# Layer 3 by row chunks, loads in pieces, value sums on VectorE and weight sums through DRAM in a four-layer graph network

## The chip, the cores and the metric

The kernel runs on one core of a Trainium2 chip. The metric is the device time of the run in microseconds; the median of several runs counts. A profiled execution gives the times of the single instructions.

## The reference

32 graphs of 512 nodes with 256 features each go through four layers. After every layer comes a residual and a layer norm over the features. The adjacency `adj` (512x512 for each graph) is the same in all layers, everything is in float32.

```python
# layer 0: x + MLP of the aggregated features
h = (1.0 + eps) * x + einsum('bnm,bmd->bnd', adj, x)
y = relu(h @ W1 + b1) @ W2 + b2
# layer 1: graph attention, 4 heads, only where adj > 0.5
h = einsum('bnd,dhf->bnhf', x, W)
e = leaky_relu(e_dst[:, :, :, None] + e_src[:, :, None, :], 0.2)
attn = softmax(where(adj > 0.5, e, -1e9)); y = einsum('bhij,bjhf->bihf', attn, h) + bias
# layer 2: 8 heads, log(adj + 1e-6) added to the scores
attn = softmax(q @ k.T / sqrt(32) + log(adj + 1e-6)); y = (attn @ v) @ Wo.T + bo
# layer 3: one head
s = (x @ W) @ x.T * adj; s = where(nodemask, s, -1e30); y = softmax(s) @ x
# after each of them
x = layernorm(x + y)
```

## The kernel before

The work is cut by graph. `prepare()` loads and turns the weights once and works out a bound that decides between `fast_path` and a general path (the general path isn't taken with these inputs). `graph(g)` then describes the four layers of one graph as small steps. 512 nodes are four chunks of 128 rows (`NC = 4`), 256 features are two chunks (`DC = 2`).

Nothing in `graph` is issued when it is described. A step has a name, an engine, an assumed duration, the steps it comes after, and the buffers it takes and frees. The class `Plan` orders them all: it keeps a simulated clock for each engine and picks among the ready steps, within a small look-ahead (`ahead`), the one whose due time is first. The due time is `max(g - 1, 0) * period` less the longest remaining chain of the step. `run` tries a few settings, takes the one that ends first by the plan's own clock, and emits the instructions of all engines in that order. Each engine then executes its own list strictly in that order, and waits where a semaphore isn't there yet. So the order of TensorE, VectorE, ScalarE, GpSimd and of SyncE's transfers is fixed when the kernel is built. Up to six graphs are under way at the same time (`"live": 6`), and steps of different layers of different graphs lie beside each other.

The buffers are a stock in SBUF by size: `B` (a 128x4x512 tile), `C` (128x4x256), single ones such as `ATd`, `dT`, `rdT`, `node`, and the eight banks of PSUM (`p`). SyncE's transfers are steps of an engine "sp" of 0.1 us, and the transfers themselves are steps of fixed length on an assumed queue.

The places that matter here, by their step names:

- Layer 0: `ldx` and `ldA` load x and the adjacency of a graph in one transfer each (L614, L619). `at` turns the adjacency on TensorE (L639), `atd` and `ate` copy it to SBUF (VectorE L643, ScalarE L647). `h` aggregates (L671), `f` and `y` are the MLP (L694, L713).
- The weights are loaded by ScalarE's queue (L320), 15 transfers at the start.
- Layer 1: `xt1` turns x (L739), and ScalarE's copy of it also sums each feature over the nodes (`xs`). `v1` makes the values (L760). `R`, `Rt`, `Re`, `Rd` make a row of exponentials, turn it, write it to DRAM (`R_dram`, L809) and read it back to all partitions (`R_bc`, L811). `z` and `zm` make the unnormalised attention (L850, L861), `o1` multiplies it with the values (L884). `hs` multiplies the feature sums with the weights (L822: four matmuls of one column, in float32 two instructions each), `hse` scales it, and `oe` adds it to the output. The sums of the weights, `d1`, come from an accumulating DMA over the chunks and one group of matmuls with ones (L930); `de` copies them to `dT` (L941), and `yt` turns, chunk by chunk, two blocks of the output and a block of `dT` (L949 to L951), so that `yn` can take the reciprocal of 4 columns (L957) and scale (L959).
- Layer 2: `s` are scores with four heads in the four row tiles of the array (L1046), `e` and `m` the exps and the products with the adjacency (L1059, L1068), `n` the outputs (L1104, column tiles). The weights of a group of four heads are summed over the chunks with two rounds of accumulating DMAs (`collect`, L1079) and then one group of matmuls with ones, `d2` (L1128). `rc` takes reciprocals (L1143), `yd` scales (L1147), `p` is the output projection (L1176).
- Layer 3: `ldA3` loads adjacency and node mask again (L1190, L1192). `i` and `t` are the similarities (L1215, L1229), `ta`, `tb`, `te` the mask, maximum and exp of one row chunk (L1243, L1249, L1257). The transposes `u` (L1274) take column block m of all four row chunks, so they come after all four exps; `w` multiplies (L1301), `wx` adds to x (L1315), then follow the norm and `out` (L1330).

Of the kernel before, what the change touches and what calls it, by code (L numbers as in the profile page):

```python
# [11 lines left out]
I32 = mybir.dt.int32  # L12
# [34 lines left out]
class Plan:  # L47
# [7 lines left out]

    HOP = {"pe": 0.2, "act": 0.15, "dve": 0.13, "pool": 0.05, "sp": 0.05}
# [3 lines left out]
        "": {"": 0.0, "row": 0.1, "c32": 0.1, "c64": 0.1},  # L60
        "row": {"": 0.13, "row": 0.1, "c32": 0.2, "c64": 0.2},
# [72 lines left out]
    def order(self, period, ahead, window, stay, shift=0.0, seed=0):  # L134
# [10 lines left out]
        rng = random.Random(seed)  # L145
        moved = {n: rng.uniform(-shift, shift) for n in [*self.steps[0], *self.steps[-1]]}
# [10 lines left out]
        while low < len(self.steps):  # L157
            found = []
            for (g, name), t in ready.items():
# [8 lines left out]
                else:  # L168
                    due = max(g - 1, 0) * period - self.left[g][name] + moved[name] + stay * change
# [47 lines left out]
def fast_path(  # L217
# [57 lines left out]
    wg_sb = const.tile([P, DC, VW], F32, name="wg_sb")  # L275
    ab_off = const.tile([P, 2, H1], F32, name="ab_off")
# [6 lines left out]
    def blk(i):  # L283
# [4 lines left out]
        "B": 14, "C": 13, "p": 8,  # L288

        "live": 6, "L0": 1, "L1": 2, "L2": 2, "L3": 1, "AT": 4, "zs": 7,  # L290
        "ATd": 1, "edge": 1, "dT": 1, "tmp": 2, "rdT": 2, "node": 1,
# [7 lines left out]
    def row(name, n):  # L299
        return tuple(f"{name}{i}" for i in range(n))  # L300


    def prepare():
# [10 lines left out]
        def load(name, us, *transfers, take=()):  # L314


            @step(f"ld_{name}", "act", 0.5 * len(transfers), take=take)
            def _():
                for transfer in transfers:
                    nc.scalar.dma_start(*transfer())  # L320

            @step(name, "q3", us, (f"ld_{name}",))
            def _():
                pass
# [4 lines left out]
        def transposed(name, w):  # L329
# [4 lines left out]
            load(f"raw{name}", 1.2, raw, take=(f"C=raw{name}",))  # L334
# [18 lines left out]
        load("eps", 2.0, lambda: (eps_bc, row_bcast(eps0, 1)))  # L353
# [3 lines left out]
        def _():  # L357
# [3 lines left out]
        load(  # L361
            "w1", 3.0, lambda: (w1_sb, rows(w1)), lambda: (b1_sb, b1.rearrange("(c p) -> p c", p=P))
        )
# [8 lines left out]
        load("bias", 3.0, *(bias_rows(k, b) for k, b in enumerate((b2, gbias, bo))))  # L372

        def vector(name, a):
# [6 lines left out]
        load(  # L381
            "wg", 3.0,
            lambda: (wg_sb[:, :, :D], wg.rearrange("(c p) h f -> p c (h f)", p=P)),
            vector("a0", a_src), vector("a1", a_dst), take=("C=a0", "C=a1"),
        )

        @step("wa", "dve", 3.2, ("wg",), take=("C=prod",), free=("prod", "a0", "a1"))
        def _():
            for k in range(2):
# [6 lines left out]
                )  # L396

# [125 lines left out]
    def graph(g):  # L523
        plan.graph()
        slot = plan.slot[-1]
        t = {"g": g}
# [4 lines left out]
        def mid(key, shape, name):  # L531
            return sb.tile(shape, F32, tag=f"C{slot[key]}", name=f"{name}_{g}")

# [24 lines left out]
        def norm_stats(n, c):  # L558
            nc.vector.bn_stats(t[f"st{n}"][:, c, :], t["x"][:, c, :])  # L559
            nc.vector.bn_aggr(t[f"mv{n}"][:, c, :], t[f"st{n}"][:, c, :])  # L560
# [5 lines left out]
        def norm_steps(n, after):  # L566


            @step(f"ve{n}", "dve", 0.09, after)
            def _():  # L570
                t["ve"] = little([P, NC], f"ve{n}")
                nc.vector.tensor_scalar_add(t["ve"], t[f"mv{n}"][:, :, 1], LN_EPS)  # L572

            @step(f"dev{n}", "pool", 1.1, (f"ve{n}",))
            def _():
                t["rstd"] = little([P, NC], f"rstd{n}")
                nc.gpsimd.tensor_tensor(t["rstd"], t["ve"], nhalf, ALU.pow)  # L577

            @step(f"sh{n}", "dve", 0.09, (f"dev{n}",))
            def _():  # L580
# [40 lines left out]
        @step("ld", "q0", 8.0, ("ldA",))  # L621
        def _():
            pass
# [1190 lines left out]
```

## Time and profile before

| | us |
|---|---|
| median of 3 runs | 3010.78 |
| lowest, highest | 3010.47, 3017.16 |
| profiled execution | 3013.04 |
| its span in the trace | 3011.3 |
| TensorE busy in it | 2944.1 |
| VectorE, ScalarE, GpSimd busy | 2009.7, 1946.5, 619.8 |
| mean granted TensorE clock | 0.991 |

The span is from the first to the last instruction of the trace; 1.7 us of the profiled execution lie around it. The profile gives for a group of instructions its line in the kernel, engine, operation, output and input names, shapes and count, then the busy time, the mean duration of one, and the idle time of that engine just ahead of it with what ended it. Durations of matmuls overlap, so the distance from the start of one group to the start of the next says what a group costs TensorE.

### The profile page before, as it was taken

To read this page: it belongs to the slowest core of one execution; us is meant where nothing else is said; L and a number is where in the kernel's file an instruction comes from. 1 tells how busy PE (TensorE), PEld (TensorE's weight loads), DVE (VectorE), ACT (ScalarE), POOL (GpSimd) and SP (SyncE) were. 2 spreads that over 40 slices of the span, in tenths; PEclk is the share of its full clock that TensorE was granted. 3 is DMA by queue.
4 is the path that set the end of the run, shared out by engine and by line. 5 is a ranking of instruction groups with operands and counts; after the bars stand their busy time and mean duration, and the time that the engine had idled before them with its cause. 6 is when DMAs were issued, how large, how long until landed. Compare 5 with 4: busy or idle time off the path is not lost. (4 is left out here: it accounts for less than half of the span.)

```text
span 3011.3 us, 40812 instructions
## 1 busy us (share of the span) xinstructions
PE 2944.1 (98%) x15053; PEld 1703.7 (57%) x15053; DVE 2009.7 (67%) x3935; ACT 1946.5 (65%) x3849; POOL 619.8 (21%) x686
## 2 busy tenths in 40 slices
PE   7899999999999999999999999999999999999996
PEld 5544655555565555565555565555565555565544
DVE  1467576676676676676676676676676676676874
ACT  2667566767666767666767666767666767666762
POOL 0222122112222112222112222112222112222210
PEclk9999999999999999999999999999999999999998
DMA  4579767788887788887787887787877787887963
GB/s 152 125 173 194 154 137 172 160 180 177 180 168 165 161 182 174 180 166 170 160 184 171 181 166 168 160 187 168 180 163 173 160 189 168 177 168 150 199 133 79
DMA packets 159782, 500.82 MB, mean 166 GB/s; under 512 B 13132, under 2 KB 48728, under 8 KB 130904
## 3 DMA queue, kind: packets, MB, share of 16 engines
q0 software_dynamic: 78336, 352.36, 62.0%
q1 hardware_dynamic: 77824, 142.88, 13.8%
q10 hardware_dynamic: 3416, 2.90, 0.3%
q8 instruction: 121, 1.98, 0.3%
q14 instruction: 85, 0.70, 0.1%
HBM read 179.06 MB, written 17.05 MB: 65 GB/s over the span
## 5 line engine op out<-in xcount | busy, mean ns | idle before, releaser
L1068 DVE SCALAR_TENSOR_TENSOR z<-AT,z 128x1024 f32<-128x1024 f32 x512 | 610.9, 1217 | 273.2 <-ACT z L1059 272.7
L1059 ACT ACTIVATE z<-s 128x512 f32<-128x512 f32 x1024 | 551.3, 611 | 268.3 <-PE s L1046 268.1
L1143 DVE RECIPROCAL rdT<-rdT 128x256 f32<-128x256 f32 x128 | 218.3, 1728 | 316.2 <-ACT rdT L1136 316.2
L861 DVE SCALAR_TENSOR_TENSOR z<-z,T,edge 128x512 f32<-128x512 f32 x512 | 357.8, 747 | 62.2 <-ACT z L850 62.0
L850 ACT ACTIVATE z<-R_bc,nT,S 128x512 f32<-128x512 f32 x512 | 382.1, 819 | 17.8 <-DMA R_bc<-R_dram 17.8
L1079 POOL DMA_DIRECT2D z<-z x192 | 169.5, 883 | 992.2 <-PE o_ps L1104 268.7
L590 ACT ACTIVATE x<-x,shift,rstd 128x256 f32<-128x256 f32 x512 | 295.4, 602 | 108.0 <-DVE shift L582 108.0
L912 POOL DMA_DIRECT2D z<-z x256 | 228.8, 1033 | 467.5 <-DMA z<-z 265.2
L1046 PE MATMUL s<-qT,kT 32*128 32x512 f32 x2048 | 291.8, 634 | 0.1
L577 POOL TENSOR_TENSOR rstd<-ve,nhalf 128x4 f32<-128x4 f32 x128 | 134.7, 1052 | 696.9 <-DVE ve L572 671.6
L1104 PE MATMUL o_ps<-z,v 128*32 128x512 f32 x2048 | 260.5, 601 | 0.3 <-ACT z L1059 0.3
L694 PE MATMUL h1T_ps<-hT,w_sb 128*128 128x512 f32 x512 | 240.0, 604 | 0.0
L1229 PE MATMUL s<-xT,iT 128*128 128x512 f32 x512 | 237.4, 598 | 0.0
L1301 PE MATMUL o_ps<-x,eT 128*128 128x256 f32 x1024 | 237.4, 385 | 0.0
L713 PE MATMUL y_ps<-w_sb,h1T 128*128 128x256 f32 x1024 | 232.4, 381 | 2.2 <-ACT h1T L700 2.2
L884 PE MATMUL o_ps<-z,v 128*64 128x512 f32 x1024 | 230.8, 602 | 1.5 <-DVE z L861 1.5
L1301 PEld LDWEIGHTS o_ps<-x,eT 128*128 128x128 f32 x1024 | 189.5, 190 | 68.1 <-issue 22.8
L713 PEld LDWEIGHTS y_ps<-w_sb,h1T 128*128 128x128 f32 x1024 | 194.6, 191 | 52.8 <-issue 20.7
L671 PE MATMUL hT_ps<-AT,x 128*128 128x384 f32 (+2 forms) x768 | 210.1, 383 | 8.8 <-ACT AT L647 8.8
L559 DVE BATCH_NORM_STATS2 st<-x 128x6 f32<-128x256 f32 x512 | 211.9, 414 | 5.6
L1046 PEld LDWEIGHTS s<-qT,kT 32*128 32x128 f32 x2048 | 93.5, 183 | 158.7 <-issue 66.8
L694 PEld LDWEIGHTS h1T_ps<-hT,w_sb 128*128 128x128 f32 x512 | 90.5, 190 | 122.0 <-issue 112.8
(145 smaller groups left out, 4261.5 us busy)
## 6 DMA issues: line engine op xcount, KB each, us to landing
z<-z POOLq DMA_DIRECT2D x192, 1024.0 KB, 8.2
A<-in_adj_dram SPq DMA_DIRECT2D x64, 1024.0 KB, 11.0
z<-z POOLq DMA_DIRECT2D x128, 512.0 KB, 8.0
x<-biases POOLq DMA_DIRECT2D x96, 512.0 KB, 9.6
R_bc<-R_dram SPq DMA_DIRECT2D x32, 1024.0 KB, 4.5
z<-z POOLq DMA_DIRECT2D x128, 256.0 KB, 7.7
x<-in_x_dram SPq DMA_DIRECT2D x32, 512.0 KB, 6.0
out_dram<-x SPq DMA_DIRECT2D x32, 512.0 KB, 3.8
```

The source lines that it names most:

```text
L590: nc.scalar.activation(t["x"][:, c, :], t["x"][:, c, :], AF.Identity, bias=t["shift"][:, c : c + 1], scale=t["rstd"][:, c : c + 1],)
L694: nc.tensor.matmul(ph, w1_sb[:, d, blk(f)], t["hT"][:, d, :], start=(d == 0), stop=(d == DC - 1))
L713: nc.tensor.matmul(py[:, j, :], t["h1T"][:, f, blk(2 * c2 + j)], w2_sb[:, f, :], start=(f == 0), stop=(f == HC - 1),)
L850: nc.scalar.activation(t[f"e{h}"][:, c, :], t["Rbc"][:, h, :], AF.Relu, bias=t["nT"][:, h, c : c + 1], scale=t["S"][:, h, c : c + 1],)
L861: nc.vector.scalar_tensor_tensor(z, z, t["T"][:, h, c : c + 1], t["edge"][:, c, :], op0=ALU.add, op1=ALU.mult)
L884: nc.tensor.matmul(po[j * F1 : (j + 1) * F1, :], t["v"][:, c, h * F1 : (h + 1) * F1], t[f"e{h}"][:, c, :], start=(c == 0), stop=(c == NC - 1),
L1046: nc.tensor.matmul(pk, t["k"][hs, o, blk(c)], t["q"][hs, o, :], start=True, stop=True)
L1059: nc.scalar.activation(t[f"E{k}"][:, j, :], t[f"ps{k}{j}"], AF.Exp, scale=QSCALE)
L1068: nc.vector.scalar_tensor_tensor(z, t["AT"][:, c, None, :].to_broadcast([P, 2, N]), ADJ_EPS, z, op0=ALU.add, op1=ALU.mult,)
L1104: nc.tensor.matmul(t[f"n{o}"][32 * j : 32 * j + 32, :], t["v2"][:, c, o * P + F2 * j : o * P + F2 * (j + 1)], t[f"E{k}"][:, j, :], start=( ...
L1229: nc.tensor.matmul(pt, t["iT"][:, d, blk(c)], t["xT3"][:, d, :], start=(d == 0), stop=(d == DC - 1),)
L1301: nc.tensor.matmul(py[:, j, :], t["eT"][:, m, blk(2 * c2 + j)], t["x"][:, m, :], start=(m == 0), stop=(m == NC - 1),)
```

## The change

1. The plan gets a stock `D` of 19 strips of 128x512; `B` falls from 14 to 11 buffers and `C` from 13 to 12. Both loads of the adjacency, the broadcast row R, layer 3's z and its transposes, `rdT`, `dT`, `ATd` and the mask live in strips.
2. The adjacency is loaded in four pieces in layer 0 and in layer 3, R in four pieces by head. `at` works on a row chunk (all column blocks of one chunk) rather than on a column block. SyncE's issues are steps of 0.4 us, and their transfers share one assumed queue `q1`.
3. The large weights are loaded by SyncE after the first graph's adjacency and x; ScalarE keeps seven small transfers. The weights of layer 1 are turned once (`wtg`, `weg`) into `wgT`.
4. `hs`: the feature sums go to DRAM (`hsi`, 256 pieces of one element), come back to all partitions (`hsbi`), and VectorE multiplies and reduces them with `wgT` (`hsl`).
5. The weight sums of layer 1 go from `dT` to DRAM (`dsi`) and back as 16 rows of 128 (`dli`); one transpose (`dt`) and one reciprocal (`rd1`) serve all four chunks. `yt` turns two blocks instead of three.
6. `yd` is done in halves, each after its own half of the reciprocals, and `p` of a pair of chunks waits only for its half.
7. Layer 3 works by row chunks: `u` turns the four blocks of one row chunk after its own exp, `w` multiplies that chunk.
8. In the last graph the weight sums of layer 2 are not collected by DMA: `d2` adds four groups of matmuls in PSUM instead of one. There the last norm and the output also go chunk by chunk, into a buffer of their own (`xo`).
9. The order: `CHANGE` has two other entries, `run` gets one setting with 13 lists of shifts (a seed each, 15% of the step names moved by up to 2 to 10 us of due time) and an earlier turn for the last graph.

The diff, cut to its core:

```diff
-        "B": 14, "C": 13, "p": 8,
-        "live": 6, "L0": 1, "L1": 2, "L2": 2, "L3": 1, "AT": 4, "zs": 7,
-        "ATd": 1, "edge": 1, "dT": 1, "tmp": 2, "rdT": 2, "node": 1,
+        "B": 11, "C": 12, "D": 19, "p": 8,
+        "live": 6, "L0": 1, "L1": 2, "L2": 2, "L3": 1, "AT": 4, "zs": 7, "edge": 1, "tmp": 2,
...
+    def transfer(name, us, after, queue="q1"):
+        @step(f"{name}.q", queue, us, after)
+        def _(): pass
+        @step(name, None, 2.0, (f"{name}.q",))
+        def _(): pass
...
-            @step(f"ld_{name}", "act", 0.5 * len(transfers), take=take)
+            @step(f"ld_{name}", "act" if little else "sp", 0.5 * len(transfers), take=take)
             def _():
                 for transfer in transfers:
-                    nc.scalar.dma_start(*transfer())
+                    (nc.scalar if little else nc.sync).dma_start(*transfer())
...
-            nc.sync.dma_start(t["A"], adj[g].rearrange("(c p) m -> p c m", p=P))
+                nc.sync.dma_start(t[f"A{c}"], adj[g].rearrange("(c p) m -> p c m", p=P)[:, c, :])
...
-                for c in range(NC):
-                    nc.tensor.transpose(pt[:, blk(c)], t["A"][:, c, blk(m)], ident)
+                for m in range(NC):
+                    nc.tensor.transpose(pt[:, m, :], t[f"A{c}"][:, blk(m)], ident)
...
-            for o in range(DC):
-                for d in range(DC):
-                    nc.tensor.matmul(
-                        ph[:, o : o + 1], wg_sb[:, d, blk(o)], t["xs"][:, d : d + 1],
-                        start=(d == 0), stop=(d == DC - 1),
-                    )
+            nc.sync.dma_start(t["xsdram"].rearrange("c p -> p c"), t["xs"])
+            nc.sync.dma_start(t["xsr"][:, 0, :], row_bcast(t["xsdram"], D))
+            for o in range(DC):
+                nc.vector.tensor_tensor_reduce(
+                    t["xsr"][:, 1, :], t["xsr"][:, 0, :], wgT[:, o, :], TINY, 0.0,
+                    op0=ALU.mult, op1=ALU.add, accum_out=t["hs"][:, o : o + 1],
+                )
...
-                nc.tensor.transpose(pt[:, 2, :], t["dT"][:, blk(c)], ident)
+            nc.sync.dma_start(t["ddram"], t["dT"][0:P:32, :])
+            nc.sync.dma_start(
+                t["dR"][: H1 * NC, :], t["ddram"].rearrange("h (c n) -> (h c) n", n=P)
+            )
+            nc.tensor.transpose(t["pdt"], t["dR"], ident)
+            nc.vector.reciprocal(t["rd1"].rearrange("p h c -> p (h c)"), t["pdt"][:, : H1 * NC])
...
-            if c % 2:
+            if c % 2 and not last:
                 collect(k, k - 1, (f"n{k-1}", f"m{k}1"))
...
+            chunks = range(a, a + NC) if last else (a,)
+                for b in chunks:
+                    for j in range(4):
+                        nc.tensor.matmul(
+                            t[f"d{o}"][32 * j : 32 * j + 32, :], ones[:, :32], t[f"E{b}"][:, j, :],
+                            start=(b == a), stop=(b == chunks[-1]),
+                        )
...
-            @step(f"u{m}", "pe", 0.44, row("te", NC) + prev("u", m), take=(f"p=u{m}",))
-                    nc.tensor.transpose(pt[:, blk(c)], t["z3"][:, c, blk(m)], ident)
+            @step(f"u{c}", "pe", 0.44, (f"te{c}",) + prev("u", c), take=(f"p=u{c}",), free=(f"z3{c}",))
+                    nc.tensor.transpose(pt[:, blk(m)], t[f"z3{c}"][:, blk(m)], ident)
...
-        plan.run([(28, 0.0, 6, 100.0, 8.0, 34035), (28, 0.05, 6, 30.0, 3.0, 427523), (28, 0.0, 6, 15.0)])
+        plan.run([(33, 0.03, 6, 15.0, ((436912, 10.0), ...), (0.7, 0.0, 0.0))])
```

## The prediction

> **What bounds the kernel now.** I read the busy shares first, then the stretches of the span, then who TensorE waited for, then its order of time at the places that the change touches.
>
> ```profile
> PE 2944.1 (98%) x15053; PEld 1703.7 (57%) x15053; DVE 2009.7 (67%) x3935; ACT 1946.5 (65%) x3849; POOL 619.8 (21%) x686
> ```
>
> TensorE is the only engine near its limit; 67 us of the span are left to it. The stretches (columns: length; busy time of TensorE, weight loads, VectorE, ScalarE, GpSimd; granted clock; DMA share; GB/s) say where these lie:
>
> ```profile
> 0.00:20.00 20.00, 4.08 (x18) 3.81 (x18) 2.18 (x12) 0.00 (x0) 0.96 (x10) 1.00 0.83 272
> 20.00:40.00 20.00, 15.49 (x61) 10.29 (x62) 3.18 (x8) 7.55 (x12) 1.06 (x1) 1.00 0.59 189
> ...
> 200.00:300.00 100.00, 94.25 (x431) 44.31 (x431) 71.11 (x118) 71.74 (x141) 27.97 (x30) 0.93 0.84 177
> ...
> 2940.00:2980.00 40.00, 28.94 (x105) 17.95 (x104) 21.81 (x46) 11.81 (x24) 2.91 (x3) 0.83 0.44 112
> 2980.00:3012.00 32.00, 18.13 (x69) 11.32 (x67) 9.77 (x27) 8.55 (x18) 1.01 (x1) 0.87 0.06 19
> ```
> ```profile
> 600.00:2700.00 2100.00, 2100.00 (x10899) 1221.89 (x10899) 1455.36 (x2837) 1406.82 (x2782) 447.08 (x490) 1.00 0.80 172
> ```
>
> From 600 to 2700 us TensorE has no idle time and the full clock: a microsecond of its work taken away there is a microsecond of the span, and no other engine's saving counts. One graph takes 90.53 us (the weight-sum matmuls come at 1040.01 and 1130.54 us). The idle time lies at the two ends, and who ended it is this (us in total, times, longest):
>
> ```profile
> PE AT_t L639 <- DMA A<-in_adj_dram: 11.6, 1, 11.6
> PE hT_ps L671 <- ACT AT L647: 8.8, 1, 8.8
> ...
> PE o2p_ps L1176 <- DVE yT L1147: 5.4, 2, 4.8
> ...
> PE fmt L493 <- DVE fmax L488: 4.8, 1, 4.8
> ...
> PE gg L472 <- DVE gm L466: 2.5, 1, 2.5
> ```
>
> **What the Trainium skill says.** "TensorE: Matmul & The Clock Gate", section "LDWEIGHTS (loading the stationary operand)": a load takes the time of its columns, about P/1.2 ns, 107 ns for 128. So a matmul of one column pays for its weights; the trace agrees: the eight one-column instructions below take 0.88 us, 110 ns each. The same page, "Part 1: The HAM clock gate": idle windows of some 3.4 us halve the clock, and about as much steady work restores it. The trace agrees: the granted clock is 0.83 and 0.87 in the last two stretches, and a matmul group after a wait at 84.94 us takes 5.35 us where one of the same 16 takes 3.65 at 93.92; so a stall costs somewhat more than its length. "DMA: Bandwidth & Descriptors", "Issuing engines are not separate DMA queues": another issuing engine saves issue time only; so the weight loads moved from ScalarE to SyncE free ScalarE, and land no faster. The same page, "Specifications": pieces under 512 B are read, changed and written. No run so far shows the price of a store of 256 four-byte pieces, which the change adds.
>
> **The change part by part.**
>
> ```profile
> 1040.01 0.95 PE L822 MATMUL hs_ps<-xs,wg_sb 128*128 128x1 f32 x8
> 1040.89 5.37 PE L884 MATMUL o_ps<-z,v 128*64 128x512 f32 x24
> ```
> ```profile
> 1167.00 0.27 PE L951 MATMUL y_t<-ident,dT 128*128 128x128 f32 x1
> 1167.11 0.39 PE L671 MATMUL hT_ps<-ATd,x 128*128 128x128 f32 x2
> ```
>
> 1. Value sums (step hs) leave TensorE: from start to next start 0.88 us (0.81 near 76.64), x32 = **-28.2 us** (ends -26 and -28.2). In their place: a store, a broadcast load, and two reductions of 256 on VectorE. Half of the 673 ns of the 512-wide reduction (L1249) plus its 83 ns read gives 0.42 each, 0.84 a graph. VectorE also splits yd (0.68 becomes about twice 0.37) and merges four reciprocals of 0.17 into one (-0.5): +0.4 us net on an engine with 31% of a 90.5 us period, 28 us, free: 0. If that cover were gone it would cost 32 x 0.4 = 13 us.
> 2. The weight sums (dT) are no longer transposed in each chunk: 4 slots of 0.11 us go, one (step dt) comes: 32 x 0.33 = **-10.6**. The new wait is d1, ScalarE copy 0.69, store, load, dt. A store of this kind (R_rows to R_dram) is issued in 0.33 and lands in 1.4 us (median; longest 5.6). I take the same for the load: 0.7 + 2 x 1.8 + hops, about 5 us. In the built order 11 us of other TensorE work stand between d1 and dt: hidden, 0. Behind a late dt stand all of TensorE's work and, on SyncE, the next loads.
> 3. TensorE's tile modes: counted in the two built orders, 697 changes of mode become 720. A change shows as 0.1 to 0.2 us in the order of time (eight row matmuls of the scores take 1.07 before a full-array group; eight of 32 columns take 0.88). More of them lead from row into column tiles, which are at the dear end: **+5** (0 to +12). The four transposes of wg: +0.4.
> 4. Start. ScalarE issues transfers until 22.55 us, then loads its table, and only then copies AT:
>
> ```profile
> 22.58 1.28 ACT L647 ACT_TABLE_LOAD   x1 [22.58 <-DMA a<-in_L_gnn_a_dst_dram]
> 23.87 2.05 ACT L647 COPY AT<-AT_t 128x512 f32<-128x512 f32 x4
> ```
>
>  After, ScalarE issues 7 transfers instead of 15; before, its seventh was issued at 11.2 us, so the copies begin between 6 and 12.5 and end 2 us later. A comes first, in four pieces, then x: 1.5 MB at the first 10 us' 235 GB/s is 6.7 us, with about 2 us of latency x is there near 9.5. So hT starts between 9.5 and 14.7, I take 14, against 24.51: **-10.5** (-8 to -13).
> 5. The bound chain of the preparation: gg stood right behind gr, fmt right behind bnd2. In the new order gg comes some 65 rows and fmt some 265 rows later. Waits of 2.5 and 4.8 go, with about 2 us of half clock: **-8** (-11 to 0, if the next late step takes their place).
> 6. End. The last graph's weight sums waited on two accumulating transfers in the chain of waits:
>
> ```profile
> 2934.05 12.76 DMA z<-z
> ...
> 2947.34 10.10 DMA z<-z
> ```
>
>  They go for six more groups of four column matmuls (0.86 each, +5.2). From the last scores (2926.70) to the end is 84.6 us now. By the new order, TensorE's work from there is 51 us at these slots, with layer 3's scores, transposes and output interleaved by chunk; some 4 for bubbles and modes; then x 0.47, statistics 0.59, ve 0.17, GpSimd 1.03, shift 0.15, ScalarE 0.6 and hops, 3.3 in all, and the output's issue to the end 5.1 as now: 64. Saved 20.6, less the three groups that come before that point (2.6): **-18** (-24 to -8). What is late next is the chain of the last chunk.
> 7. Loads in pieces: 20 SyncE issues a graph instead of 7, 13 x 0.36 = 4.7 us more on a queue that mostly waits, hidden while its order fits. DMA gains about 400 packets a graph beside 5000, and stands at a share of 0.80. B falls from 14 to 11 buffers, but A, A3, R, z3 and eT leave it, so z and E have no fewer. Layer 3's interleaving moves copies and exps, adds no work: 0 in the middle. For stalls that these moves bring I take **+5** (0 to +70).
>
> Sum: -28.2 - 10.6 + 5.4 - 10.5 - 8 - 18 + 5 = -65. The profiled execution took 3013.0 us (span 3011.3 and 1.7 around it), so 2948; the median of the runs, 3010.8, lies 2.3 lower: **2946 us**.
>
> **The rivals.** *Only the work goes*: the ends keep their stalls in other places; then items 1 to 3 alone count, -33, and 2977 us. For it: a plan made for other durations can move a stall; against it: the seven transfers and the removed accumulations are plain in the order. *A late weight sum*: both small transfers land like the slowest R_dram store, 5.6; 0.7 + 2 x 5.9 = 12.5 against 11.2, some 1.3 us a graph and a little clock, 45 us, and 2990. For it: the DMA engines stand at 0.80; against: the median of 1.4 was measured under this load. *SyncE's queue stops the pipeline (slower)*: an issue waits at the head of the one ordered queue, and everything behind it is late. Right before the weight sums' store stands an old graph's output, and SyncE waited 1022 us in 30 such waits for ScalarE's last norm. If that norm comes after d1 by more than the 6 us between the chain and its cover, TensorE stops each graph. It decides from 65/31 = 2.1 us of stop a graph; at 4 us it is +124 - 65, 3070 us. Against it: waiting at the head costs nothing as long as the order of events is the order of the queue. *Nothing done*: loads of weights for hs were hidden and the ends unchanged: 3011; the slot of 0.88 speaks against it.
>
> **How the numbers follow.** Forecast 0.62 (own range 2920 to 2965), only the work 0.15, late sum 0.10, queue 0.10, nothing 0.03. About 0.3% is what a measurement of this kernel can tell from no change. Faster: 0.62 + 0.15 + 0.10 = 0.87; within: 0.03; slower: 0.10. The range goes from 2920 (all ends good) to 2995 (late sum and its bound); what is left out is the queue, nothing, and some 0.05 below.
>
> **What would show it.** Right: the period falls from 90.5 to about 89.5 and TensorE stays without idle time from 600 to 2700; no hs_ps; hT's second group before 15 us; no wait of fmt or gg; about 64 us from the last scores to the end. Wrong: idle time of TensorE in the middle, ended by a d_rows load, R_bc or A; a DMA share near 1; hT still near 24 us; longer slots of the column groups.

## The result and the profile after

| | before | after |
|---|---|---|
| median of 4 runs, us | 3013.62 | 3407.07 |
| lowest, highest | 3010.47, 3017.16 | 3403.80, 3411.37 |
| profiled span | 3011.3 | 3406.0 |
| mean granted clock | 0.991 | 0.938 |

The ratio is 1.131 (95% interval 1.1285 to 1.1327): the kernel is slower by 393 us, where 65 less were predicted. The first part of the page after:

```profile
PE 2996.1 (88%) x14753; PEld 1692.0 (50%) x14753; DVE 2054.4 (60%) x4133; ACT 1934.0 (57%) x3818; POOL 653.6 (19%) x685
```

TensorE issues 300 matmuls fewer, as the sum had it, and is idle for 410 us instead of 67. The waits of TensorE (us in total, times, longest):

```profile
PE R_t L851 <- ACT R L834: 347.5, 28, 13.3
PE o_ps L951 <- DVE z L927: 14.4, 5, 5.4
...
PE d_t L1032 <- DMA d_rows<-d_dram: 8.9, 2, 6.1
...
PE AT_t L690 <- DMA A<-in_adj_dram: 5.0, 1, 5.0
```

One wait, in 28 of the 32 graphs, makes 347 of the 410 us. It names ScalarE's R, which only passed on what it waited for. The chain of waits at one such place (start, length, what):

```profile
1515.18 14.96 DMA xs_dram<-xs
...
1530.19 4.72 DMA xs_row<-xs_dram
...
1534.93 0.43 DVE xs_row L893
...
1535.90 0.12 DVE ab L826
...
1536.05 0.22 ACT R L834
...
1536.32 0.38 PE R_t L851
```

TensorE in order of time, at the same place:

```profile
1521.88 1.88 PE L1340 MATMUL s<-xT,iT 128*128 128x512 f32 x4
1536.32 0.38 PE L851 MATMUL R_t<-ident,R 128*16 128x128 f32 x1 [12.55 <-ACT R L834]
...
1537.35 3.62 PE L1340 MATMUL s<-xT,iT 128*128 128x512 f32 x4
```

The wait costs more than its length. The same four score matmuls take 1.88 us before it and 3.62 behind it; two stretches of the span (columns as in the prediction) show the clock granted there, 1.00 and then 0.50:

```profile
1520.00:1525.00 5.00, 3.77 (x16) 2.19 (x14) 0.69 (x4) 2.09 (x6) 0.00 (x0) 1.00 1.09 177
1536.00:1541.00 5.00, 4.68 (x11) 2.50 (x12) 1.48 (x5) 1.94 (x7) 0.00 (x0) 0.50 0.89 227
```

Over the whole run TensorE is busy for 52 us longer than before, with less work. Experiment 9 below has the same 14753 matmuls and hardly waits, and there they take 2905 us, not 2996.

The first line of the chain is the store of the value sums, 256 pieces of four bytes. SyncE waits for its landing before it issues the load of the row. VectorE's reductions (L893) wait for the row. Behind them in VectorE's fixed order stands `ab`, a small sum for the attention scores, which needs nothing of the value sums; behind `ab` come ScalarE's `R` and TensorE's `R_t`, and behind `R_t` all of TensorE. The plan gives this store 0.4 us and 2.0 to land, and the row the same. The time from the issue to the landing, for the 15 of the 32 stores of which the trace tells it:

```profile
DMA to landing us min/median/max: 13.2/16.2/17.1
```

From the issue of the store to that of the row's load, for which SyncE needs the landing, it is 14.8 us (median of all 32). The first graph's store is slow too, with one transfer of 512 KB beside it:

```profile
46.57 0.38 SPq L878 DMA_DIRECT2D xs_dram<-xs  x1
58.16 0.33 SPq L885 DMA_DIRECT2D xs_row<-xs_dram  x1
```

Some of the expectations below take 15.5 us for the store; that is the median of a view which has three of the row's loads (5.0 us) among the stores. ScalarE waits only 30 us for R's load in this run. The period, from one store of R to the next (8th to 30th), is 105.05 us after and 90.53 before.

### The profile page after: what moved, and what is told of

The parts are those of the page before. It is cut to its first block, busy times and chain, and to the rows that moved or that the text cites. A ratio compares the mean times of both kernels' runs of the same rounds, so it can differ in the third digit from the quotient of the medians.

```text
span 3406.0 us, 41454 instructions
## 1 busy us (share of the span) xinstructions
PE 2996.1 (88%) x14753; PEld 1692.0 (50%) x14753; DVE 2054.4 (60%) x4133; ACT 1934.0 (57%) x3818; POOL 653.6 (19%) x685
## 4 chain that ended last, share of the span: by engine, by line
PE 75%; DMA 20%; ACT 3%; DVE 1%; issue 1%; SPq 0%; POOL 0%; ACTq 0%; POOLq 0%; DVEq 0%
DMA xs_dram<-xs 13%; PE s L1139 8%; PE o_ps L951 7%; PE o_ps L1197 7%; PE hT_ps L723 7%; PE h1T_ps L746 6%; PE o_ps L1394 6%; PE y_ps L765 6%; DMA xs_row<-xs_dram 4%; PE v_ps L1120 3%; PE kT_ps L1102 3%; PE iT_ps L1326 3%; PE o2p_ps L1282 3%; PE s L1340 3%; PE qT_ps L1102 3%; PE d_ps L1227 2%
## 5 line engine op out<-in xcount | busy, mean ns | idle before, releaser
L916 ACT ACTIVATE z<-R_bc,nT,S 128x512 f32<-128x512 f32 x512 | 395.1, 817 | 30.1 <-DMA R_bc<-R_dram 30.1
L618 POOL TENSOR_TENSOR rstd<-ve,nhalf 128x4 f32<-128x4 f32 (+1 forms) x131 | 174.5, 1332 | 1056.2 <-DVE ve L612 880.4
L851 PE MATMUL R_t<-ident,R 128*16 128x128 f32 x32 | 11.8, 369 | 347.5 <-ACT R L834 347.5
L636 ACT ACTIVATE x<-x,shift,rstd 128x256 f32<-128x256 f32 x508 | 282.0, 601 | 46.8 <-DVE shift L626 46.7
L1340 PE MATMUL s<-xT,iT 128*128 128x512 f32 x512 | 285.1, 689 | 0.0
L893 DVE CUSTOM_DVE_ANT_0 xs_row<-xs_row,wgT 128x256 f32<-128x256 f32 x64 | 27.2, 425 | 426.3 <-DMA xs_row<-xs_dram 425.2
L951 PE MATMUL o_ps<-z,v 128*64 128x512 f32 x1024 | 250.8, 610 | 14.4 <-DVE z L927 14.4
L834 ACT ACTIVATE R<-ab 128x16 f32<-128x16 f32 x32 | 6.9, 216 | 375.7 <-DVE ab L826 375.7
L1394 PEld LDWEIGHTS o_ps<-x,eT 128*128 128x128 f32 x1024 | 197.2, 196 | 42.7 <-ACT eT L1384 11.5
```

What stands on the lines that cost most here:

```text
L916: nc.scalar.activation(t[f"e{h}"][:, c, :], t[f"R{h}"], AF.Relu, bias=t["nT"][:, h, c : c + 1], scale=t["S"][:, h, c : c + 1],)
L951: nc.tensor.matmul(po[j * F1 : (j + 1) * F1, :], t["v"][:, c, h * F1 : (h + 1) * F1], t[f"e{h}"][:, c, :], start=(c == 0), stop=(c == NC - 1),
L1340: nc.tensor.matmul(pt, t["iT"][:, d, blk(c)], t["xT3"][:, d, :], start=(d == 0), stop=(d == DC - 1),)
L1394: nc.tensor.matmul(py, t[f"eT{c}"][:, blk(m)], t["x"][:, m, :], start=(m == 0), stop=(m == NC - 1),)
```

## The experiments

Times are medians. The kernel before, measured beside them, had 3011.7 to 3013.6.

**1. Is it the store?** The row keeps its place but is loaded from the bias; no store, all other orders as after.

```diff
-            nc.sync.dma_start(t["xsdram"].rearrange("c p -> p c"), t["xs"])
+            pass
-            nc.sync.dma_start(t["xsr"][:, 0, :], row_bcast(t["xsdram"], D))
+            nc.sync.dma_start(t["xsr"][:, 0, :], row_bcast(gbias, D))
```

> The changed kernel without the store of the feature sums in 256 four-byte pieces; the row is loaded from the bias in its place, so the value sums are not the real ones. All engines keep their order. Theory (the landing of that store, 15 us, holds the row's load on SyncE, so VectorE's reductions, so ab, R and R_t behind them): the row lands 5 us after the sums are ready, before VectorE's turn; no wait at R_t, the period falls from 105.3 to about 89.5 us, time 2920 to 2970 us. Rival (the 20 issues a graph of SyncE or the loads in pieces hold the pipeline, the store is one symptom): R_t stops waiting but other waits of 5 us a graph or more come in its place, time above 3100 us.

3171.72 us (ratio 1.054, 1.0521 to 1.056). The wait for `R_t` is gone and 235 us with it: the store is the larger part. But the kernel stays 160 us over before, so it is not all. What TensorE and ScalarE wait for now:

```profile
PE o_ps L1393 <- ACT eT L1383: 79.0, 29, 4.9
PE h1T_ps L746 <- ACT hT L730: 45.9, 26, 2.0
```
```profile
ACT z L915 <- DMA R_bc<-R_dram: 256.5, 35, 10.5
```

ScalarE in order of time shows how the second makes the first:

```profile
1517.96 0.60 ACT L1383 COPY eT<-eT_t 128x512 f32<-128x512 f32 x1
1527.83 1.52 ACT L915 ACTIVATE z<-R_bc,nT,S 128x512 f32<-128x512 f32 x2 [9.27 <-DMA R_bc<-R_dram]
1529.26 0.56 ACT L1383 COPY eT<-eT_t 128x512 f32<-128x512 f32 x1
```

The copy of eT at 1529.26, for which TensorE waits, needs nothing of R; it stands behind the activations that do. It is the same fault in another queue.

**2. Fewer, longer pieces.** The row is stored as 128 pieces of eight bytes; orders of TensorE and VectorE unchanged.

```diff
-            t["xsdram"] = dram.tile([DC, P], ...); nc.sync.dma_start(t["xsdram"].rearrange("c p -> p c"), t["xs"])
+            t["xsdram"] = dram.tile([P, DC], ...); nc.sync.dma_start(t["xsdram"], t["xs"])
```

> The same sums stored as they lie, 128 pieces of 8 bytes instead of 256 of 4; the order on all engines is kept and VectorE reads the row in the other order. Theory (each small piece waits its turn beside the accumulating transfers' packets, so the landing goes with the number of pieces on each DMA engine, 8 instead of 16): landing from 15.5 to about 8 us, TensorE's wait at R_t from 12.5 to about 5 us, time about 3170 us (3100 to 3250). Rival (a fixed time for a store from 128 partitions under load): landing stays at 15, time 3400 us.

3278.93 us (1.088). VectorE reads the row in the other order. The store lands in 9.4 us (median) instead of 16.2, and the wait for `R_t` falls from 347 to 230 us. Half the pieces take 3.9 us off the period.

**3. Take the reductions out of the way.** They move to the first eviction that uses them, some 78 VectorE instructions later.

```diff
-        @step("hsl", ...): two tensor_tensor_reduce
+        ... the same two, emitted in step oe0
```

> The store stays in 256 pieces and as slow as it was; only VectorE's two reductions of each graph stand later in VectorE's order, right ahead of where ScalarE adds the value sums to the output (oe), behind ab. TensorE's and SyncE's orders are kept. Theory (the harm is what stands behind the wait on VectorE): the store still lands in 15 us, R_t no longer waits for R; SyncE still holds R_rows' store behind the row's load, so R lands some 7 us later than in the run without the store, covered by 35 us of TensorE work between R_t and its use: 2930 to 3010 us. Rival (SyncE's one queue passes the lateness on): the first z of layer 1 wait for R_bc and TensorE stops at the outputs of layer 1 by 5 us a graph or more, time above 3100 us.

3266.81 us, far from the 2930 to 3010 expected. No wait for `R_t`, but SyncE still stood 431 us in 32 waits for the store's landing, with the store and load of R behind it, and ScalarE's and VectorE's waits moved on: `eT_t <- DVE ATd` is now TensorE's largest, 123 us.

**4. Tell the plan.** `hs` lands 15 us after its issue and `hsb` 4.6; the order is made anew with the same setting.

> The instructions of the change, but the plan is told that the store of the sums lands 15.4 us after its issue and the row 5 us after its own (2.4 us each before), so it orders everything anew by its own rules. Theory (a wrong duration in the plan is the whole cause): the reductions move behind ab and the row's load behind R's store, no wait at R_t, 2920 to 2990 us. Rival (an order made anew by shifts that were found for another plan has stops of its own): 3000 us or more with waits spread over several lines.

3193.59 us: the rival's side. The store is out of the way; ScalarE's wait for R is still 230.7 us in 34 times. 1, 3 and 4 each take the store away from TensorE and stay 160 us or more above before, with the same wait: my theory of one cause falls.

**5 and 6. Why does R land late?** In 1, SyncE issues R's four pieces among eight pieces of the adjacencies (the same size), x and the node mask. First the piece of layer 3's A ahead of R goes behind it; then all of A3, A and x go behind the output's store, some 45 us away.

```diff
-            ... Rsi, ldni, lb0i, Rl0i..Rl3i, lb1i.., la0i..la3i, lxi, out0i
+ (5)        ... Rsi, ldni, Rl0i..Rl3i, lb0i, lb1i.., la0i..la3i, lxi, out0i
+ (6)        ... Rsi, ldni, Rl0i..Rl3i, out0i, lb0i.., la0i..la3i, lxi
```

> Edit on e1_no_store (the store of the value sums left out, the row read from the bias instead, so the sums are not the real ones): in SyncE's order the first piece of layer 3's A is moved behind the four pieces of R, which it stood ahead of. The orders of TensorE, VectorE, ScalarE and GpSimd stay those of e1. Theory (what is left of the loss, some 160 us or 5 us a graph, is R's row landing late: in e1 ScalarE waits for it 256.5 us in 35 waits, where the plan lets the rows be there 5.4 us after the issue): if a piece that was issued first is also served first, R lands 1.3 to 3 us earlier and the kernel gains 30 to 90 us, 3080 to 3140. If the pieces issued behind it (4 of A3, 4 of A, x: 2.5 MB within 10 us) share the engines with it, the gain is nothing, 3150 to 3180. Rival (ScalarE and VectorE are late on their own, in layer 3's chunks): no change either, and the next run tells the two apart.

> Edit on e1_no_store (value sums not the real ones): layer 3's four pieces of A, the next graph's four pieces of A and its x, 2.5 MB that SyncE issues around R's four pieces and that are used 75 to 87 us later in the plan, are moved behind the store of the output, some 35 us later in the plan. R's four pieces and the node mask stay. The other engines' orders are those of e1. Theory (R lands late since it shares the transfer engines with 2.5 MB that nobody needs yet): ScalarE's wait for R falls from 256 us to under 60, TensorE's waits for ScalarE's copies of e and h (79 + 46 + 16 us) mostly go, the period falls from 97 to about 91 us, and the time to 2940 to 3010. Rival (ScalarE or VectorE is late on its own, in layer 3's chunks): ScalarE's wait for R may fall, TensorE's waits stay under other names, and the time stays over 3100.

3166.23 and 3163.97 us: nothing, in both. Loads issued around R are not what delays it. In 6 the node mask (256 KB) and GpSimd's accumulating transfers are left beside R. SyncE and GpSimd in order of time in 6:

```profile
1505.48 0.33 SPq L889 DMA_DIRECT2D R_dram<-R_rows  x1
...
1510.96 1.75 SPq L898 DMA_DIRECT2D R_bc<-R_dram  x4
```
```profile
1495.97 1.14 POOL L1199 DMA_DIRECT2D z<-z  x1
1511.46 1.04 POOL L1199 DMA_DIRECT2D z<-z  x1 [14.35 <-DMA z<-z]
```

Layer 2's merge of 1 MB issued at 1495.97 is done at 1511.4, and the next starts as R's load starts. R's store takes 5.5 us until the load can be issued, and ScalarE gets R at 1523.5. In the kernel before, GpSimd's next merge comes when R is nearly back:

```profile
1089.54 0.33 SPq L809 DMA_DIRECT2D R_dram<-R_rows  x1
```
```profile
1094.43 0.86 POOL L1079 DMA_DIRECT2D z<-z  x1 [9.14 <-PE o_ps L1104]
```

Added up from the records of the DMA engines, layer 2's merges take 82% of the engines' time in the 6 us behind R's store in 1 and 6, and nothing in before (medians of 25 graphs). The new order has put them there.

**7 and 8. The sums late, or back on TensorE, with the loads apart.** 7 is 3 with 6's order and the row's load behind R; 8 puts the four products back on TensorE in the bank of the last value product.

> Edit on e3_reduce_later (VectorE's sums at the first eviction that needs them, some 78 of its instructions later; all sums real): the loads of A3, A and x moved behind the output's store as in e6_loads_apart, and the load of the row of sums moved behind R's four pieces, so that SyncE no longer stands 14 us before the store of R for the landing of the 256 pieces. The other engines' orders are those of e3. Theory (two late landings, the store's and R's, make the whole loss, and neither is in TensorE's way now): 2940 to 3020, with the store's landing still 14 to 16 us and nobody waiting for it. Rival (there is a third cause in the order of ScalarE or VectorE): over 3100.

> The value sums back on TensorE, as in the kernel before (four products of one column behind the last value product, in the same bank, and ScalarE's scaling): no store, no row, no sums on VectorE; the rest of the change stays, with the loads of A3, A and x behind the output's store as in e6_loads_apart. Theory: e6_loads_apart plus TensorE's price for the four products, 28 us over the kernel by the trace of before, so 2970 to 3030, about the kernel before. If it is level with e6_loads_apart, the products were not worth the row's way through memory at all. Rival (a third cause): over 3100.

3194.26 and 3180.74 us. Both keep ScalarE's wait for R (235.7 and 221.3 us). Without any store of the sums, 8 is no better: this second cause has nothing to do with the value sums.

**9. Take the suspected cost away.** 6 with the last two of layer 2's six merges carrying an eighth of their bytes.

```diff
+                if k >= 6:
+                    src, dst = src[:, : N // 2], dst[:, : N // 2]
```

> Edit on e6_loads_apart (value sums not the real ones): the last two of layer 2's six merges of 1 MB (z added into z by GpSimd's DMAs; blocks 6 and 7), which are in flight while the rows of R are stored and read back, carry an eighth of their bytes, so layer 2's weight sums are not the real ones either. All four engines' orders and SyncE's stay. Theory (e6 took the loads away and R still landed some 10 us after its issue, against 4.5 in the kernel before, because the merges hold the transfer engines at that moment: in e6 a merge is issued 9 us and another 6 us around the store of R): R's store lands in 2 to 3 us and not 5.5, R in about 5 and not 10, ScalarE's wait for R falls from 237 us to under 60 and the time from 3164 to 2950 to 3010. Rival (R's rows land late for another reason, such as their four pieces): no change, 3150 to 3180. Second rival (the wait for R goes and TensorE still waits as long for ScalarE's copies): over 3100 with R landing in 5.

2939.02 us (0.976, 0.9742 to 0.9772). SyncE, ScalarE's wait for R, and the middle of the span:

```profile
1498.25 0.33 SPq L889 DMA_DIRECT2D R_dram<-R_rows  x1
...
1500.13 1.75 SPq L898 DMA_DIRECT2D R_bc<-R_dram  x4
```
```profile
ACT z L943 <- DMA R_bc<-R_dram: 17.5, 13, 2.7
```
```profile
600.00:2700.00 2100.00, 2098.89 (x10691) 1200.08 (x10690) 1498.84 (x2996) 1408.51 (x2777) 472.71 (x488) 1.00 0.70 153
```

R's load is issued 1.9 us after its store, TensorE is busy from 600 to 2700 us, and 225 us are gone. The merges beside R are the second cause; it shows only where the first is away, since in the kernel after ScalarE waits 30 us for R.

**10. The same from the other side.** The merges keep their bytes; R's pieces are read from other rows in memory, without waiting for R.

```diff
-                ... row_bcast(t["Rdram"][h * NC : (h + 1) * NC, :], N)   # after Rs
+                ... row_bcast(biases[0:1, 0:2], N)                       # ahead of Rsi
```

> Edit on e6_loads_apart (value sums not the real ones): the four pieces of R are read from the rows of biases in memory instead of the stored R, and are issued ahead of R's store, some 10 us earlier in the plan, so nobody waits for R's way through memory; layer 1's weights are not the real ones. The other engines' orders stay, and the merges keep their size. Theory (the late landing of R is all that is left of the loss, through ScalarE's fixed order: its copies of e and h stand behind the activations that read R): 2940 to 3010, no wait of ScalarE for R to speak of, TensorE's waits for the copies of e and h mostly gone. Rival (ScalarE is late on its own): over 3100.

3047.30 us: 117 of the 225. The rest is a wait that my edit made: the four loads held SyncE's queue for 11.7 us, the node mask behind them came late (VectorE waited 85.1 us for it) and `ATd` behind the mask (TensorE, 68.1 us). So the run supports the theory without measuring its size.

**13. One cause or two?** The kernel after, store and all, with four merges (2, 5, 6, 7) cut to an eighth.

> The kernel after with one edit: the merges of blocks 2, 5, 6 and 7 of layer 2, which are in flight from the store of the value sums until R has been read back, carry an eighth of their bytes (layer 2's weight sums are not the real ones); the store of 256 four-byte pieces, the row and all orders stay as they are. Theory (one cause: the merges, bunched by the new order, slow both transfers that TensorE stands behind): the store lands in 5 us and not 15.5, R in about 5, the wait for R_t falls from 347 us to under 80, and the time to 2940 to 3030. Rival (two causes: 256 pieces are slow by themselves): the store still takes over 10 us, the wait for R_t stays over 200 us, and the time is 3150 to 3250.

3210.02 us. The wait that remains, and the store's landings:

```profile
PE R_t L851 <- ACT R L834: 191.3, 28, 7.7
```
```profile
DMA to landing us min/median/max: 8.7/9.5/12.9
```

Two causes. With the merges small the store still takes 9.5 us; the merges add 5 to 7 to it (16.2 less 9.5 by the landings, 14.8 less 9.5 by the issues of the row). It shares the engines with a 512 KB bias transfer then, so its price alone is not settled; in no run did a store of 256 pieces, where the trace tells its landing, take under 7.5 us (14).

**11, 12 and 15. The value sums alone, in the kernel before.** Its order of TensorE is kept, less the four products; the four transposes for `wgT` come in at the start, and the node mask is loaded into the tile in which it is turned. In 11 the store is issued when the sums are there; in 12 behind R's load, and the row ahead of layer 3's A; in 15 as in 12, but the first five graphs and the last keep their products.

```diff
-                    nc.tensor.matmul(ph[:, o : o + 1], wg_sb[:, d, blk(o)], t["xs"][:, d : d + 1], ...)
+                nc.vector.tensor_tensor_reduce(t["phs"], t["xsr"], wgT[:, o, :], TINY, 0.0, ...)   # at hse
+ (11)      store in xe11, row behind R_bc;   (12) store behind R_bc, row ahead of A3
+ (15)      (12) for 5 <= g < B - 1 only
```

> The kernel before with one part of the change done alone: layer 1's value sums on VectorE. The store of 256 four-byte pieces is issued when the sums of x are there, the row is read back right behind R's load some 20 us later, and the two reductions stand in VectorE's order where ScalarE's scaling of the sums stood, some 60 us after the store; the orders of TensorE, ScalarE and GpSimd are those of before without the four products a graph and the scaling. (To make room the node mask is turned in its own tile, and the products of the reduction go to the bank the sums had.) Theory (the store's landing of 15 us costs nothing where 60 us of other work lie between it and its reader; the part is worth TensorE's time, 28 us): 2980 to 2992 against before's 3012, no wait for the row. Rival (the store or the row delays other transfers, of A or R, or the products were hidden anyway): 3005 to 3060.

> The part of e11_before_sums_on_VectorE once more, with SyncE's order mended: there the store of the sums stood ahead of layer 0's A, and TensorE waited 466 us for A, since SyncE stood at the store for the sums (1116 us) where it had run ahead before. Here the store is issued behind R's load and the row is read back just ahead of layer 3's A, some 20 us later; the orders of the four other engines are those of e11. Theory (a part that takes its time from TensorE and whose landing is covered by 20 to 60 us gives its 28 us): 2980 to 2995, no wait for the row and none for A beyond before's 12 us. Rival (SyncE stands for the store's landing, 15 us, and layer 3's A comes late): 3010 to 3100, with a wait of TensorE or VectorE for A. Second rival (the products were hidden): 3008 to 3015.

> The part of e12_before_sums_late_store for the 26 graphs of the steady stretch (the sixth to the last but one); the first five and the last keep their four products on TensorE and store nothing. In e12 the distance between two stores of R fell from 90.5 to 89.7 us for most graphs, the 0.8 us of TensorE that the part takes away, but the start came 10 us later (VectorE stood 8.9 us for the first graph's row, and the second A was issued behind the store's landing) and the end lost it again (VectorE stood 11.2 us for the last row). Theory (the part is worth its TensorE time wherever its landing is covered): 26 times 0.8 us less than before's 3012, so 2986 to 2996. Rival (the gain of the period is taken back elsewhere, at the edges, whatever is done there): 3005 to 3020.

11: 3518.92 us, worse than the kernel after. SyncE now stood at the store for the sums, 1116 us in all, and layer 0's A, which it had issued ahead of time before, stood behind:

```profile
PE AT_t L650 <- DMA A<-in_adj_dram: 466.3, 26, 19.2
```

12: 3018.45 us, no gain (1.0017, 1.0009 to 1.0026). The distance between two stores of R fell from 90.5 to 89.7 us for most graphs, but VectorE waited 8.9 us at the start, and 11.2 us for the last row at the end. At the start:

```profile
87.39 0.43 DVE L852 CUSTOM_DVE_ANT_0 hs_ps<-xs_row,wgT 128x256 f32<-128x256 f32 x1 [8.85 <-DMA xs_row<-xs_dram]
```

15: 3002.16 us, ratio 0.9957 (0.9944 to 0.9969). The period is 89.8 us on the mean; from the 6th store to the last it gains 22.5 us. It gains less than expected, since the start is still late: its 6th store of R comes 10.4 us after that of before (the profiled execution was 4 us over the median). No row is used there yet. One lead, not tested: VectorE waits 12.3 and 8.8 us for the node mask at 205 and 304 us, where before has one such wait, of 5.5 us, in this stretch, so it may be the mask's shared tile.

**14. Tell the plan everything.** The kernel after with its plan told what its trace shows, and shifts chosen for that.

```diff
+    LANDS = {"hs": 15.0, "hsb": 5.0, "Rs": 5.0, "Rl": 7.0, "ds": 5.5, "dl": 5.0, "la": 5.0, "lb": 5.0, "lx": 5.0, "ld": 5.0}
+        merges' queue time x1.15; pieces of A 1.5 and of R 1.2 us on theirs; other 25 shifts,
+        look-ahead 0.3 for 0.03, weight of a mode change 35 for 15
```

> The kernel after with the plan told what the transfers took in its trace: the store of the sums lands 15 us after its issue, the row 5, R's store 5, R's pieces 7, the loads of A and x 5, the weight sums' store and load 5.5 and 5, and GpSimd's merges hold their queue 15% longer; the whole order is made anew with shifts chosen for these figures. Nothing is left out. The plan's own end is 2974 us (2900 for the kernel after with its own figures, 2958 for the kernel before, which took 3012). Theory (the loss is landings that the plan did not know; told, it keeps other work ahead of them): 2990 to 3080, with no wait of ScalarE for R over 100 us and none for R_t. Rival (the slow landings are made by the order itself, since it bunches merges, and move to other transfers in a new order): over 3100.

3015.92 us (1.0016, 1.0007 to 1.0025): nothing left out, nothing taken back to TensorE, and all of the loss but 2.6 us is gone. ScalarE's wait for R, and the middle of the span:

```profile
ACT z L930 <- DMA R_bc<-R_dram: 11.2, 5, 4.2
```
```profile
600.00:2700.00 2100.00, 2082.62 (x10417) 1156.02 (x10415) 1451.82 (x2915) 1388.94 (x2702) 450.47 (x478) 1.00 0.82 171
```

The loss was the order's: the same work in another order doesn't have it. Which part of the new order does it is not separated. It was made for longer landings, but the landings changed with it: the store lands in 8.0 us (median), where 15 was told, and no merge is in flight in the 6 us behind R's store (0%, counted as above). The look-ahead, the weight of a mode change and the shifts are new as well. But the gain is gone too: the period is 92.3 us, with 0.8 of it idle, so TensorE is busy for longer with less work. In the built order its tile modes change 931 times, against 720 in the kernel after; at the 0.1 to 0.2 us of a change that is 0.7 to 1.3 us a graph. The rest, up to 0.8 us a graph over experiment 9's 90.0, isn't explained.

**16. The start's queue.** 15 with the weights' loads issued by SyncE.

```diff
-                    nc.scalar.dma_start(*transfer())
+                    nc.sync.dma_start(*transfer())
```

> e15_before_sums_26_graphs, and the loads of the weights issued by SyncE, not by ScalarE, as in the kernel after, in the order in which the plan has them. In before ScalarE loads its table at 22.58 us, behind the issue of the weights, and TensorE's first product of layer 0 starts at 24.51; in the kernel after, with this and the pieces of A, they are at 7.27 and 11.32. Theory (ScalarE's issuing is what held the start, by itself): the first product starts at 13 to 17 us and the time is 7 to 12 us below e15. Rival (A lands later with the weights on the same queue, or the weights come late for layer 0's second product): no gain, or up to 10 us slower than e15.

3000.40 us (0.9952, 0.994 to 0.9964). The theory holds for the start: TensorE's first product of layer 0 that reads ScalarE's copy of AT begins at 14.22 us, not 24.51 (the very first, on VectorE's copy, at 13.90, not 15.04). But the first store of R comes where it came in before (0.4 us earlier), so nearly all of it is lost again before then; against 15 the gain is 1.8 us, within the scatter of the two, where 7 to 12 were expected. Of the versions that compute everything, 15 and 16 alone are faster than the kernel before, by 0.4 to 0.5%.

## Why the prediction was wrong

The time predicted, 2946 us, is nearly that of experiment 9; the order that gives it stands on transfers that 9 had to shrink. Even there the match is in part luck: of 9's gain some 34 us come from the start, where the sum had 18.5, some 0.5 us a graph from the steady middle, where it had 1.0, and the rest, some 26, from the end, where it had 18.

- **Item 1, value sums.** Its TensorE part was nearly right: 0.74 to 0.8 us a graph measured (12, 15) for 0.88. The step that failed is "on an engine with 31% of a 90.5 us period, 28 us, free: 0". It weighed VectorE's busy time, 0.4 us, and neither the row's landing nor what stands behind the waiting reduction. The landing was 20 us for store and row together (15.0 and 4.7 in the chain), and VectorE's share of busy time says nothing of it: without the store 235 us are gone (1). The bound of 13 us for a lost cover was sized by the busy time too. The text said that no run showed the price of such a store, and then carried no bound for it into the sum.
- **Item 2, weight sums.** Right that it is hidden: TensorE waited 8.9 us for `d_rows`, in 2 waits. Its size was off: SyncE could issue the load 6.2 us (median) after the store, where 1.8 was taken from R's store; the cover of 11 us took it up.
- **Item 3, tile modes.** Too small. In 9 the period is 90.0 us; the value sums alone give 89.8 (15). With the weight sums' 0.33 it should be 89.5, so 0.5 us a graph went to something in the order, against 0.16 that the sum had for the modes; the runs did not separate what.
- **Items 4 and 5, start.** Right at their places. The table load and the first product of layer 0 on AT after:

```profile
7.27 1.28 ACT L700 ACT_TABLE_LOAD   x1 [7.27 <-DMA A<-in_adj_dram]
```
```profile
11.32 0.91 PE L723 MATMUL hT_ps<-AT,x 128*128 128x384 f32 x2 [1.98 <-ACT AT L700]
```

 14 us were predicted. The waits of gg and fmt are gone. In 9 the 8th store of R comes 38.0 us earlier than before, some 4 of it by the shorter period; items 4 and 5 had 18.5. But 16 shows that an early first product alone brings little: the order behind it decides.
- **Item 6, end.** From the last scores at 3345.01 us to the end are 61.0 us, 64 predicted, 84.6 before.
- **Item 7, loads and stalls.** "+5 (0 to +70)" is the second step that failed. The loads in pieces around R are harmless (5, 6). The order placed layer 2's merges beside the store of the sums, where cutting four of them saved 197 us (13), and beside the store and load of R, where ScalarE had no slack: 225 us once the first store is gone (9).
- **The rival of SyncE's queue** had the mechanism of one late step stopping each graph, but at another place (the weight sums' store behind the output), and priced it at 4 us a graph; the period rose by 14.5.

Of the signs I had named, the idle time in the middle came true. A DMA share near 1 did not: from 600 to 2700 us it is 0.72, against 0.80 before. A mean share says nothing of the moment in which the one urgent transfer lands: in the stretch of the store it is 1.00.

```profile
1515.00:1530.00 15.00, 8.77 (x32) 5.22 (x30) 5.38 (x16) 3.57 (x11) 1.34 (x2) 0.93 1.00 184
```

What the sum had no term for is the clock: the waits made the matmuls themselves some 90 us longer (2996 against 2905 us). The prediction had said that a stall costs more than its length; for the middle of the span it forecast none.

The Trainium skill, "DMA: Bandwidth & Descriptors", section "Queues, rings and completion order", says that a DMA engine takes turns between the queues that have work for it, a packet from each, and works one queue's ring in order. The runs agree with the first part: what GpSimd's queue carried beside R made 225 us (9). Of the second they show only that loads behind R on its own queue made no difference (6), nor a piece of 256 KB taken from ahead of it (5). I had read the neighbouring section, on issuing engines, for issue time only.

## What to carry to other kernels

Price a small transfer by its landing beside the traffic of its moment, and then read what stands behind its reader in that engine's fixed order: 0.8 us of VectorE work behind a store of 1 KB took 12.5 us from TensorE in nearly every graph, and full clock for some time behind it. An order that is tuned to a plan's own figures puts no slack where those figures are wrong; an order made with the landings of a trace lost next to nothing (14), though the run doesn't show that the figures alone did it. Look, too, at which large transfers the order lays beside the urgent ones. When work moves off the bounding engine, give its result a reader far away (15), and look at what the queue of its transfer would have done ahead of time (11).

## What the runs showed of the hardware

- A store of 1 KB in 256 four-byte pieces landed in 7.5 us at the least (14), in 9.5 (median) beside lighter traffic (13), in 10.3 in the kernel before (12), and in 16.2 beside 1 MB accumulating transfers (after); with 128 pieces of eight bytes it was 9.4 in that place (2). R's 8 KB, 16 rows of 512 bytes, landed in 1.4 us (median) in the kernel before.
- The store and load of R on SyncE's queue were slowed by accumulating transfers on GpSimd's queue (R's 8 KB store 5.5 us until its load could be issued, against 1.9 with the merges cut), and not measurably by 2.5 MB of loads on its own queue around it (5, 6).
- Behind a wait of 12.55 us the granted clock was 0.50 (1536 to 1541 us), and four matmuls took 3.62 us that took 1.88 before it.
